# A two-layer graph network on one core: attention in blocks of 512 queries, exponentials over four tiles, and a block's order written as one string

## The chip, the cores and the metric

The kernel runs on one core of a Trainium2 chip. The time is device time in microseconds, from the launch of the program on the core to its end. Every run of the kernel before is given; the median of the three is the number that the change is compared with. The profile is of one more execution of the same program.

The core has five instruction streams that run side by side and wait for one another by semaphores: TensorE (PE, with its weight loads shown apart as PEld), VectorE (DVE), ScalarE (ACT), GpSimd (POOL) and SyncE (SP, which here only issues DMAs). Each stream does its instructions in the order in which the program gives them, so one that waits holds up all that stand behind it on its engine.

## The reference

`x` is 3327 x 128, `adj` is a 3327 x 3327 matrix of zeros and ones. Layer 0 is a graph convolution with a batch norm and layer 1 an attention with `adj` added twice to its scores. Layer 1 takes almost all of the time:

```python
h = max(layernorm(x), 0)
q = (h @ Wq.T).reshape(128, 3327, 8)      # 128 batches d, 3327 nodes n, 8 features h
k = (h @ Wk.T).reshape(128, 3327, 8)
v = (h @ Wv.T).reshape(128, 3327, 8)
a = einsum('dnh,dmh->dnm', q, k) * 128 ** -0.5
a = softmax(a + adj + adj, axis=2)
out = einsum('dnm,dmh->dnh', a, v).reshape(3327, 1024)
x = x + out @ Wo.T
```

So there are 128 independent attentions over 3327 nodes, each with only 8 features, and 128 x 3327 x 3327 exponentials (1.4 thousand million).

## The kernel before

Layer 0 and the first projections fill about the first 260 us of the profile. Everything after is `attention()`.

**Tiles.** The nodes are padded to NP = 3328 = 26 key chunks of 128. Four batches (G = 4) are worked at a time, which makes 32 groups `i`. Inside a group the queries are cut into blocks `y` of QB = 480: six of 480 and a last one of 448. For one key chunk `c` and one half of the four batches (`half`, two batches) there is one *pair*: two score matmuls (`product`, L804), one for each batch, into a PSUM tile `s` of two banks (bank x takes batch x of the half). The contraction has 32 rows (8 features, each as two parts of query and key), so batch b sits on rows 32b to 32b+31 of the array. A block has 26 x 2 = 52 pairs, a group 7 x 52 = 364, each of 960 (or 896) columns on 128 partitions.

**Two ways through a pair.** Chunks 0 to 17 (`WC = 18`) are *plain*: DVE adds the adjacency tile `at` to the scores and writes a slice of a tile `d` (`add`, L939), and ACT later takes exp(2x) over the whole `d` in place (`late`, L984). Chunks 18 to 25 are *weighted*: ACT takes exp(2x) straight from PSUM into a tile `f` (`weighted`, L948), and POOL multiplies `f` by a tile `wt` of exp(2 adj) that was stored in DRAM (`wd`) beforehand (L951). Either way the pair ends in SBUF, and four matmuls in four column groups (`weigh`, L686) multiply two pairs by the values and a column of ones into the accumulator bank `av`.

**Steps.** A block is 13 steps (`SU = NC // 2`) of four pairs. Ten steps have three plain pairs and one weighted, and the three steps in `DOUBLE = (3, 7, 11)` have two of each. The text of a step fixes the order on every engine:

```python
weighted(rest[0][0], coming)          # score product, exp (ACT), multiply (POOL)
late()                                # ACT: exp over the d of the step before, 2 or 3 pairs
add(0, product(...)); second(0)       # DVE add; PE: four weigh matmuls, three steps behind
add(1, product(...))
add(2, product(...))                  # or a second weighted()
second(1)
```

**Buffers.** PSUM is full: `psc` has three `s` tiles of two banks, used in turn by every `product` whichever kind it is, and two banks hold `av`, one for each of two blocks in turn. In SBUF there are four `d` (three pairs each), six `f`, four `at` (two chunks each) and three `wt` (one chunk each). A product therefore waits until the pair three places before it has been read, by DVE if that was plain and by ACT if it was weighted.

**Beside it.** `fetch(x + PRE)` issues the `at` and `wt` DMAs from SP two steps ahead. `finish` (L696 to L720) turns a finished block's `av` on DVE, divides it and stores it; its parts are placed at the steps in `PARTS`. `loads` brings the next group's q, k and v, with POOL sorting k (`sort`, L193), spread over the group. `begin` and `go_on` place ten small pieces in a group (six projections of a later part of layer 1 and four of the output product; L209 to L295): a matmul into the idle `av` bank, a copy on DVE, and for q and k two more instructions on POOL and DMAs from SP. `more_weights` does exp on chunks 24 and 25 of the next block's `wd`, in the first group only.

Of the kernel before, what the change touches and what calls it, by code (L numbers as in the profile page):

```python
# [9 lines left out]
F32 = mybir.dt.float32  # L10
# [11 lines left out]
P = 128  # L22
NC = 26
# [3 lines left out]
QB = 480  # L27
# [4 lines left out]
SU = NC // 2  # L32
# [4 lines left out]
DOUBLE = (3, 7, 11)  # L37
PARTS = (3, 7, 8)
# [9 lines left out]
def tile_two_layer_gnn(  # L48
# [73 lines left out]
    PRE = 2  # L122

    FROM = [3 * SU] + [LAG + 1] * (NG - 1)

# [565 lines left out]
    def finish(rp, av, d0, n0, w):  # L691
# [10 lines left out]
        ri = av[:, QB : QB + J]  # L702
# [22 lines left out]
    def attention():  # L725
# [3 lines left out]
        with tc.tile_pool(name="exd", bufs=4) as ep, tc.tile_pool(  # L729
            name="adj", bufs=4  # L730
        ) as ap, tc.tile_pool(name="adw", bufs=3) as wp, tc.tile_pool(
            name="exf", bufs=6
# [7 lines left out]


# [4 lines left out]
            if True:  # L746
                steps = [
                    (i, y, s)
                    for i in range(NG) for y in range(len(qblocks)) for s in range(SU)
                ]  # L750

                def at(i):
                    return i * G

                def pairs(s):


                    return kinds[s]

                kinds = []  # L760
                for s in range(SU):
                    j, k = (sum(len(x[i]) for x in kinds) for i in range(2))
                    n = 2 if s in DOUBLE else 1
                    kinds.append((
                        [(x // 2, x % 2) for x in range(j, j + 4 - n)],
                        [(WC + x // 2, 1 - x % 2) for x in range(k, k + n)],
                    ))


                wanted, have = [], {}  # L770
                for x, (i, y, s) in enumerate(steps):
                    n0, w = qblocks[y]
                    for c, _ in pairs(s)[0]:
                        if (0, i, y, c // 2) not in have:
                            have[0, i, y, c // 2] = None
                            wanted.append((x, 0, i, y, c // 2))
                    for c, _ in pairs(s)[1]:
                        if (1, i, y, c) not in have:
                            have[1, i, y, c] = None
                            wanted.append((x, 1, i, y, c))  # L780

                def fetch(x):
                    while wanted and wanted[0][0] <= x:
                        _, kind, i, y, c = wanted.pop(0)
                        n0, w = qblocks[y]
                        if kind:
                            a = wp.tile([P, QB], F32, name="wt")
                            nc.sync.dma_start(a[:, :w], wd[c - WC, :, n0 : n0 + w])
                        else:
                            a = ap.tile([P, 2, QB], F32, name="at")  # L790
                            n = min(2, WC - 2 * c)
                            nc.sync.dma_start(
                                a[:, :n, :w], adjr[:, 2 * c : 2 * c + n, n0 : n0 + w]
                            )
                        have[kind, i, y, c] = a

                def product(i, y, c, half):
                    q, k, _ = sets[i % 2]
                    n0, w = qblocks[y]
                    we = w + w % 2  # L800
                    p = psc.tile([P, 2, NB], F32, name="s")
                    for x in range(2):
                        rs = slice(64 * half + 32 * x, 64 * half + 32 * x + 32)
                        nc.tensor.matmul(  # L804
                            p[:, x, :we], k[rs, c, :], q[rs, n0 : n0 + we],
                            start=True, stop=True,
                        )
                    return p

                waiting, ending, pending = [], [], []  # L810
                others = [
                    args for b in range(G)
                    for args in q_loads(sets[0][0], 32 * b, b, NB, NP - NB)
                ]
                late = None

                def more_weights(i, y, s):

                    if i or y + 1 >= len(qblocks) or s not in (1, 8, 12):
                        return  # L820
                    n0, w = qblocks[y + 1]
                    if s == 1:
                        have["w"] = wk.tile([P, 2, QB], F32, name="t4")
                        nc.sync.dma_start(
                            have["w"][:, :, :w], adjr[:, WC + NW :, n0 : n0 + w]
                        )
                    a = have["w"][:, :, :w]
                    if s == 8:
                        nc.scalar.activation(a, a, AF.Exp, bias=low, scale=2.0)
                    if s == 12:  # L830
                        nc.sync.dma_start(
                            wd[NW:, :, n0 : n0 + w].rearrange("c p n -> p c n"), a
                        )

                extra, begun = [], []

                def begin(i, y, s):
                    if extra and s in DOUBLE[1:]:  # L840
                        begun.append(extra.pop(0))
                        drive(begun[0], avs2[(i * len(qblocks) + y + 1) % 2])

                def go_on(i, y, s):
                    if begun and s in DOUBLE:
                        drive(begun[0])
                    elif begun:
                        drive(begun.pop(0))
                    for j in [1, 2] if i == 0 else [i + 2] if i + 2 < NG else []:
                        if (y, s) != (2 * (j - 1) if i == 0 else 0, 3):  # L850
                            continue
                        hj = wk.tile([P, CH], F32, name="hj")
                        nc.sync.dma_start(hj, hd[:, j * CH : (j + 1) * CH])
                        extra.extend(projections(wk, hj, j, False, ov, low_half[:CH, 1:2]))
                    if (y, s) == (2, 12) and i:
                        extra.extend(outputs(wk, i - 1))

                def second(part):

                    if not due:  # L860
                        return
                    (i, y, s), es = waiting[0]
                    n0, w = qblocks[y]
                    av = avs2[(i * len(qblocks) + y) % 2]
                    ps = sum(pairs(s), [])
                    for j in (0, 1) if part == 0 else (2, 3):
                        c, half = ps[j]
                        for x in range(2):
                            weigh(
                                sets[i % 2], av, w, es[j][:, x, :w], 2 * half + x, c,  # L870
                                s == 0 and part == 0, s == SU - 1 and part == 1,
                            )
                    if part:
                        waiting.pop(0)
                        if s == SU - 1:
                            ending.append(finish(rp, av, at(i), qblocks[y][0], w))

                def step():
                    for g in ending[:1]:
                        if next(g, g) is g:  # L880
                            ending.pop(0)

                def first(x):
                    i, y, s = steps[x]
                    return product(i, y, *pairs(s)[1][0])

                def first_loads():

                    q, k, v = sets[0]
                    ks = sets[1][1].rearrange("p c n -> p (c n)")  # L890
                    for b in range(G):
                        for args in k_loads(ks, 32 * b, b, 0, NP):
                            nc.sync.dma_start(*args)

                    for b in range(G):
                        for args in q_loads(q, 32 * b, b, 0, NB):
                            nc.sync.dma_start(*args)
                    for args in v_loads(v, 0):
                        nc.sync.dma_start(*args)

                    for c, copy in (
                        (16, nc.scalar.copy), (0, nc.vector.tensor_copy),
                        (4, nc.gpsimd.tensor_copy), (8, nc.scalar.copy),
                        (20, nc.vector.tensor_copy), (12, nc.gpsimd.tensor_copy),
                        (24, nc.vector.tensor_copy),
                    ):
                        n = min(4, NC - c)
                        copy(
                            k[:, c : c + n, :],
# [286 lines left out]
```

## Time and profile before

| | |
|---|---|
| runs | 10039.32, 10042.86, 10046.28 us; median 10042.86 |
| profiled execution | span 10038.4 us from its first to its last instruction; no other time is recorded for it, and the three runs lie 0.9 to 7.9 us above this span |
| busy: ACT, PE, DVE, POOL | 9869.9 (98%), 9683.1 (96%), 9306.6 (93%), 8455.3 us (84%) |
| TensorE clock granted | 0.995 of full speed as a mean |
| attention: first and last DVE add | 268.8 and 10010.9 us |
| instructions of the four main lines | L939 DVE 8064, L951 POOL 3584, L984 ACT 2912, L948 ACT 3584 |

A row of the groups reads: line, engine, operation, output tile <- input tiles, partitions x elements of output and input, count, then busy time in all and the mean of one, then the time the engine sat idle just before such an instruction and what ended most of that. The record of one instruction can overlap that of the next on its engine; busy time counts such a stretch once, the mean counts it in both. Matmuls are pipelined, so PE's busy share is not its share of peak.

### The profile page before, as it was taken

How to read it: one execution, taken by the hardware profiler on the slowest of the kernel's cores; microseconds unless marked ns; L12 is line 12 of the kernel's file. 1: busy time of each engine (PE TensorE's matmuls, PEld its weight loads, DVE VectorE, ACT ScalarE, POOL GpSimd, SP SyncE). 2: the span in 40 equal slices, each digit the busy share in tenths (PEclk: the TensorE clock that was granted, in tenths of full speed). 3: DMA queues.
4: the chain of work that ended last, by engine and by line, in shares of the span. 5: the costliest groups of instructions: out<-in, count | busy, mean ns of one | idle time of the engine just before them, and what ended most of it. 6: DMA issues, size and time to landing. Idle time of an engine off the chain costs nothing. (4 is left out here: it accounts for less than half of the span.)

```text
span 10038.4 us, 187289 instructions
## 1 busy us (share of the span) xinstructions
PE 9683.1 (96%) x71535; PEld 2727.4 (27%) x71535; DVE 9306.6 (93%) x9527; ACT 9869.9 (98%) x6649; POOL 8455.3 (84%) x4331
## 2 busy tenths in 40 slices
PE   8899999999999999999999999999999999999998
PEld 3222222222222222222222222222222222222222
DVE  5899999999999999999999999999999999999998
ACT  5999999999999999999999999999999999999999
POOL 1788888888888888888888888888888888888887
PEclk9999999999999999999999999999999999999999
DMA  7766666666666666666666666666666666666654
GB/s 296 197 181 170 168 168 174 173 172 167 165 173 174 172 169 167 166 175 174 171 167 170 167 171 176 169 169 167 169 175 172 172 166 167 171 175 172 161 156 131
DMA packets 1035388, 1735.65 MB, mean 173 GB/s; under 512 B 126926, under 2 KB 1009356, under 8 KB 1025132
## 3 DMA queue, kind: packets, MB, share of 16 engines
q1 hardware_dynamic: 1031975, 1718.70, 62.4%
q8 instruction: 562, 9.21, 0.4%
q0 software_dynamic: 784, 4.03, 0.1%
q14 instruction: 351, 2.87, 0.1%
q10 hardware_dynamic: 1716, 0.85, 0.0%
HBM read 1620.93 MB, written 102.27 MB: 172 GB/s over the span
## 5 line engine op out<-in xcount | busy, mean ns | idle before, releaser
L939 DVE SCALAR_TENSOR_TENSOR d<-at,s 128x960 f32<-128x960 f32 x8064 | 8730.2, 1138 | 430.2 <-PE s L804 291.0
L951 POOL TENSOR_TENSOR f<-f,wt 128x960 f32<-128x960 f32 (+1 forms) x3584 | 7936.6, 2233 | 1339.1 <-ACT f L948 1305.4
L984 ACT ACTIVATE d<-d 128x2880 f32<-128x2880 f32 (+1 forms) x2912 | 7071.9, 2429 | 6.9 <-DVE d L939 4.8
L686 PE MATMUL av<-d,v 128*9 128x480 f32 x32256 | 5050.8, 565 | 0.6 <-ACT d L984 0.6
L804 PE MATMUL s<-q,k 32*128 32x480 f32 x23296 | 4236.3, 475 | 288.5 <-ACT f L948 210.9
L948 ACT ACTIVATE f<-s 128x960 f32<-128x960 f32 (+1 forms) x3584 | 3445.0, 988 | 18.4 <-issue 8.7
L804 PEld LDWEIGHTS s<-q,k 32*128 32x128 f32 x23296 | 1806.3, 182 | 5528.9 <-DVE d L939 3409.2
L686 PE MATMUL av<-f,v 128*9 128x480 f32 x14336 | 2842.4, 565 | 0.0
L686 PEld LDWEIGHTS av<-d,v 128*9 128x9 f32 x32256 | 584.2, 88 | 1204.8 <-issue 1203.1
L686 PEld LDWEIGHTS av<-f,v 128*9 128x9 f32 x14336 | 317.4, 88 | 153.6 <-issue 140.0
L193 POOL CAST k<-ks 128x256 fp32r<-128x256 f32 x434 | 284.0, 654 | 0.0
L517 PE MATMUL acc<-a,A 128*128 128x512 f32 (+1 forms) x364 | 159.1, 591 | 22.7 <-DMA a<-in_adj 22.7
L240 POOL TENSOR_TENSOR o<-pf,o 104x512 fp32r<-104x512 f32 x124 | 159.8, 1289 | 9.9
L696 DVE STREAM_TRANSPOSE avs<-av 128x480 f32<-128x480 f32 (+1 forms) x224 | 149.3, 667 | 4.4 <-PE av L686 4.4
L527 DVE TENSOR_REDUCE amax<-a 128x1 f32<-128x3327 f32 x26 | 93.7, 3605 | 53.9 <-DMA a<-in_adj 53.9
L495 POOL TENSOR_SCALAR heavy<-heavy 128x3328 f32<-128x3328 f32 x6 | 17.8, 2960 | 128.5 <-DMA heavy<-in_adjT 80.3
L517 PEld LDWEIGHTS acc<-a,A 128*128 128x128 f32 x364 | 71.5, 200 | 113.7 <-issue 97.9
L524 ACT ACTIVATE junk<-a 128x3327 bf16<-128x3327 f32 x26 | 77.3, 2972 | 19.9 <-DMA a<-in_adj 19.9
L238 DVE TENSOR_SCALAR pf<-av,low_half 104x512 f32<-104x512 f32 x62 | 46.5, 751 | 37.4 <-PE av L209 36.3
L236 DVE COPY pf<-av 104x512 f32<-104x512 f32 x62 | 42.9, 691 | 39.5 <-PE av L209 38.8
L239 POOL CAST o<-pf 104x512 fp32r<-104x512 f32 x124 | 76.0, 613 | 0.0
L215 DVE COPY ov<-av 104x512 f32<-104x512 f32 x62 | 42.9, 691 | 33.4 <-PE av L209 33.3
(133 smaller groups left out, 913.7 us busy)
## 6 DMA issues: line engine op xcount, KB each, us to landing
at<-in_adjT SPq DMA_DIRECT2D x1728, 480.0 KB
wt<-wd SPq DMA_DIRECT2D x1536, 240.0 KB
at<-in_adjT SPq DMA_DIRECT2D x288, 448.0 KB
wt<-wd SPq DMA_DIRECT2D x256, 224.0 KB
ks<-kT SPq DMA_DIRECT2D x496, 104.0 KB
q<-qT SPq DMA_DIRECT2D x496, 104.0 KB
a<-in_adj SPq DMA_DIRECT2D x26, 1663.5 KB
kT<-o SPq DMA_DIRECT2D x128, 208.0 KB
```

Of the source, the lines that this page charges most:

```text
L193: nc.gpsimd.tensor_copy(k[:, c : c + n, half * 64 : half * 64 + 64], ks.bitcast(F32).rearrange("g (p c) -> g c p", c=NC)[:, c : c + n, :],)
L240: nc.gpsimd.tensor_tensor(o[:CH, 1], f[:CH], of[:CH, 0], ALU.subtract)
L517: nc.tensor.matmul(acc[i][:, :w], A[:, c, :], a[:, n0 : n0 + w], start=(c == 0), stop=(c == NC - 1),)
L524: nc.scalar.activation(junk, a[:, :N], AF.Copy, accum_out=deg[:, c : c + 1])
L527: nc.vector.tensor_reduce(amax[:, c : c + 1], a[:, :N], AX.X, ALU.max, apply_absolute_value=True)
L686: nc.tensor.matmul(av[32 * b : 32 * b + H + 1, :w], tiles[2][:, b, c, :], e, start=first, stop=last,)
L696: nc.vector.transpose(avs[:, :J, :].rearrange("p j h -> p (j h)"), av[:, : 32 * J].rearrange("p (q j) -> p j q", j=J),)
L804: nc.tensor.matmul(p[:, x, :we], k[rs, c, :], q[rs, n0 : n0 + we], start=True, stop=True,)
L939: nc.vector.scalar_tensor_tensor(d[:, j, :, :w], have[0, i, y, c // 2][:, c % 2, :w] .unsqueeze(1).to_broadcast([P, 2, w]), SAFE / 2, p[:, ...
L948: nc.scalar.activation(f[:, :, :w], p[:, :, :w], AF.Exp, scale=2.0)
L951: nc.gpsimd.tensor_tensor(f[:, :, :w], f[:, :, :w], have[1, i, y, c][:, :w].unsqueeze(1).to_broadcast([P, 2, w]), ALU.mult,)
L984: nc.scalar.activation(flat, flat, AF.Exp, scale=2.0)
```

## The change

The block is now 512 queries: six blocks of 512 and a last one of 256. In the last one two key chunks lie side by side in a tile, so that every tile of scores, and every instruction on one, has 2 x 512 columns. A block of 512 has 52 such tiles and the block of 256 has 26. `RUN = 4` plain tiles share a `d`, so the exponential over `d` has 4096 columns. There are three `d` instead of four (each larger by a third and by 512/480), and five `f` instead of six.

The steps are gone. A string names what comes next, one for the blocks of 512 (`WIDE`) and one for the last (`NARROW`): `A` a plain tile, `B` a weighted tile, `L` the exponential over the oldest full `d`, `v` the value matmuls of the oldest couple of tiles of one kind, `F` and `G` parts of `finish`, `P` the matmul of one of the small pieces and `E` the rest of it (its DMAs come at the next `L`). A `v` lies six couples behind (`BEHIND`). `at` and `wt` tiles are fetched by how many tiles of their kind have gone by (`AHEAD`); a `wt` tile of the last block holds two chunks. In `finish` the reciprocal is written over the first columns of `av`, since the bank is now full. The diff, cut to its core (what the removed steps did is described above):

```diff
-QB = 480
+QB = 512
-SU = NC // 2
-DOUBLE = (3, 7, 11)
-PARTS = (3, 7, 8)
+RUN = 4
+BEHIND = 6
+AHEAD = ((8, 3), (4, 2))
+WIDE = (
+    "LAAvABvvABvAAvALAvFBBvABAvAALAvB"
+    "AvALAvGBvBAAvLAAvvBAvALAvPABAvAA"
+    "LvvABBvBEALAvAAPvBLAAvAAvBvBE"
+)
+NARROW = "ABvAAAvLvBAvAAAvLvBBFvABAvAALvABALvAAvvBGABALv"
...
-        ri = av[:, QB : QB + J]
+        ri = av[:, :J]
...
-        with tc.tile_pool(name="exd", bufs=4) as ep, tc.tile_pool(
+        with tc.tile_pool(name="exd", bufs=3) as ep, tc.tile_pool(
...
-            name="exf", bufs=6
+            name="exf", bufs=5
...
+NY = len(qblocks)
+many = [QB // w for _, w in qblocks]
+orders = [WIDE if m == 1 else NARROW for m in many]
+def items(kind, y):
+    first, units = ((0, WC), (WC, NC - WC))[kind]
+    m = many[y]
+    return [
+        (first + u * m, half ^ kind) for u in range(units // m) for half in (0, 1)
+    ]
...
+def fetch(kind, ahead):
+    queue = wanted[kind]
+    while (
+        issued[kind] < len(queue)
+        and queue[issued[kind]][0] <= number[kind] + ahead
+        and issued[kind] <= max(current[kind], 0) + AHEAD[kind][1]
+    ):
...
+def product(i, y, c, half):
+    q, k, _ = sets[i % 2]
+    n0, w = qblocks[y]
+    p = psc.tile([P, 2, NB], F32, name="s")
+    for e in range(many[y]):
+        for x in range(2):
+            rs = slice(64 * half + 32 * x, 64 * half + 32 * x + 32)
+            nc.tensor.matmul(
+                p[:, x, e * w : (e + 1) * w],
+                k[rs, c + e, :], q[rs, n0 : n0 + w],
+                start=True, stop=True,
+            )
+    return p
...
+def put(kind, i, y, item):
+    couple[kind].append(item)
+    if len(couple[kind]) == 2:
+        quads.append((i, y, list(couple[kind])))
+        couple[kind].clear()
+def exponentials():
+    d, n = full.pop(0)
+    flat = d[:, :n].rearrange("p j x n -> p (j x n)")
+    nc.scalar.activation(flat, flat, AF.Exp, scale=2.0)
+def second():
+    i, y, two = quads.pop(0)
+    n0, w = qblocks[y]
+    m = many[y]
+    av = avs2[(i * NY + y) % 2]
+    z = done[i, y] = done.get((i, y), -1) + 1
+    end = orders[y].count("v") - 1
+    for e in range(m):
+        for c, half, t in two:
+            for x in range(2):
+                weigh(
+                    sets[i % 2], av, w, t[:, x, e * w : (e + 1) * w],
+                    2 * half + x, c + e, z == 0 and e == 0,
+                    z == end and e == m - 1,
+                )
+    if z == end:
+        ending.append(finish(rp, av, at(i), n0, w))
...
+def plain(i, y, j):
+    c, half = items(0, y)[j]
+    fetch(0, AHEAD[0][0])
+    number[0] += 1
+    current[0] += j % 4 == 0
+    p = product(i, y, c, half)
+    if not open_:
+        open_.append(ep.tile([P, RUN, 2, QB], F32, name="d"))
+    d, z = open_[0], len(open_) - 1
+    open_.append(j)
+    nc.vector.scalar_tensor_tensor(
+        d[:, z],
+        have[0, i, y, j // 4][:, j // 2 % 2]
+        .unsqueeze(1).to_broadcast([P, 2, QB]),
+        SAFE / 2, p, ALU.min, ALU.add,
+    )
+    if z + 1 == RUN or j + 1 == len(items(0, y)):
+        full.append((d, z + 1))
+        open_.clear()
+    put(0, i, y, (c, half, d[:, z]))
+def weighted(i, y, j):
+    c, half = items(1, y)[j]
+    fetch(1, AHEAD[1][0])
+    number[1] += 1
+    current[1] += j % 2 == 0
+    p = product(i, y, c, half)
+    f = fp.tile([P, 2, QB], F32, name="f")
+    nc.scalar.activation(f, p, AF.Exp, scale=2.0)
+    nc.gpsimd.tensor_tensor(
+        f, f,
+        have[1, i, y, j // 2].unsqueeze(1).to_broadcast([P, 2, QB]),
+        ALU.mult,
+    )
+    put(1, i, y, (c, half, f))
...
+        for token in orders[y]:
+            if token == "A":
+                plain(i, y, z[0])
+                z[0] += 1
+            elif token == "B":
+                weighted(i, y, z[1])
+                z[1] += 1
+            elif token == "L":
+                if full:
+                    exponentials()
+                for part in then:
+                    part()
+                then.clear()
+            elif token == "F":
+                step()
+            elif token == "G":
+                step()
+                then.append(step)
+            elif token == "P":
+                if extra:
+                    begun.append(extra.pop(0))
+                    drive(begun[0], avs2[(i * NY + y + 1) % 2])
+            elif token == "E":
+                if begun:
+                    drive(begun[0])
+                    then.append(lambda part=begun.pop(0): drive(part))
+            else:
+                if i * total_v + v >= BEHIND:
+                    second()
+                if v == start and i + 1 < NG:
+                    pending = loads(sets[(i + 1) % 2], at(i + 1), ksp)
+                    total = len(pending)
+                while pending and (total - len(pending)) * (
+                    total_v - start - 10
+                ) <= (v - start) * total:
+                    pending.pop(0)()
...
```

## The prediction

> **What bounds the kernel now.** First the page's busy shares, then busy time by stretch, to see whether ACT's 98% is 98% everywhere.
>
> ```profile
> PE 9683.1 (96%) x71535; PEld 2727.4 (27%) x71535; DVE 9306.6 (93%) x9527; ACT 9869.9 (98%) x6649; POOL 8455.3 (84%) x4331
> ```
> ```profile
> 0.00:250.00 250.00, 201.22 (x506) 94.38 (x507) 146.06 (x246) 137.95 (x144) 47.39 (x61) 0.91 0.79 297
> ...
> 1000.00:5000.00 4000.00, 3896.18 (x29220) 1080.55 (x29212) 3767.04 (x3818) 3998.59 (x2672) 3463.45 (x1765) 1.00 0.63 170
> 5000.00:9000.00 4000.00, 3895.80 (x29230) 1082.16 (x29226) 3766.74 (x3821) 3998.78 (x2673) 3460.47 (x1762) 1.00 0.63 170
> ```
>
> Columns: stretch, length, busy us (count) of PE, PEld, DVE, ACT, POOL, then clock, DMA share, GB/s. ACT idles 2.6 us in 8000, so the attention lasts as long as ACT's instructions do. PE's 97% is not such a bound: the timeline has eight value matmuls in 0.99 us and four score matmuls in 0.49 to 0.89, about 2.5 of the 3.34 us of a step; the rest is waiting.
>
> ACT's price per instruction comes from starts in its timeline (start, record length, what):
>
> ```profile
> 5013.71 2.61 ACT L984 ACTIVATE d<-d 128x2880 f32<-128x2880 f32 x1
> 5016.21 1.83 ACT L948 ACTIVATE f<-s 128x960 f32<-128x960 f32 x2
> 5017.91 1.83 ACT L984 ACTIVATE d<-d 128x1920 f32<-128x1920 f32 x1
> 5019.60 0.99 ACT L948 ACTIVATE f<-s 128x960 f32<-128x960 f32 x1
> 5020.45 2.64 ACT L984 ACTIVATE d<-d 128x2880 f32<-128x2880 f32 x1
> ```
>
> From start to next start: 2.50 us for 2880 columns, 0.85 for an `f` of 960, 1.69 for 1920. Records are longer than this because they overlap. Means over 1500 to 3500 us: 2.502 (2880), 2.339 (2688), 1.695 (1920), 1.590 (1792), `f` 0.850 (960) and 0.796 (896). The slope over the `d` rows is 0.838 ns a column (it is 0.82 to 0.85 between neighbours), which leaves 0.085 us fixed in each `d`.
>
> Next to ACT stands DVE; its rows and what it and PE wait for:
>
> ```profile
> L939 DVE SCALAR_TENSOR_TENSOR d<-at,s 128x960 f32<-128x960 f32 x6912 | 7546.5, 1148 | 330.9 <-PE s L804 206.3 <-issue 21.0 <-ACT d L984 0.8
> L951 POOL TENSOR_TENSOR f<-f,wt 128x960 f32<-128x960 f32 x3072 | 6864.9, 2253 | 1161.6 <-ACT f L948 1128.3 <-DMA wt<-wd 7.4
> ```
> ```profile
> PEld s L804 <- DVE d L939: 3409.2, 5381, 1.6
> PEld s L804 <- ACT f L948: 1302.6, 1792, 2.0
> DVE d L939 <- PE s L804: 291.0, 604, 2.6
> ACT f L948 <- PE s L804: 6.6, 7, 1.5
> ```
>
> Score matmuls wait for DVE or ACT to free a PSUM tile, DVE waits now and then for scores, ACT almost never.
>
> **The change part by part.** *ACT.* Counts in a group: before, 91 `d` (60 of 2880, 18 of 1920, 10 of 2688, 3 of 1792) and 112 `f` (96 of 960, 16 of 896); after, from the strings, 58 `d` of 4096, one of 2048, and 104 `f` of 1024. The columns are the same, 346,112. Before: 60x2.502 + 18x1.695 + 10x2.339 + 3x1.590 + 96x0.850 + 16x0.796 = 303.2 us (5345 ACT instructions in 8000 us are 26.33 groups of 203, so 303.8 was seen). After, a `d` of 4096 is 2.502 + 1216 x 0.000838 = 3.52, of 2048 1.80, an `f` 0.904: 204.2 + 1.8 + 94.0 = 300.0. Saved: 3.1 a group, 98 us in 32. The Trainium skill (ScalarE: Activation LUTs, What ACT_TABLE_LOAD costs) has 0.833 ns a column and 186 ns fixed less 93 of overlap: 93 x 1280 instructions fewer (40 a group) = 119 us. With its column price the trace leaves (303.8 - 288.4)/203 = 76 ns fixed as a mean, not 93: 97 us. I take the trace. Bounds: 73 us if the 1216 columns past 2880 cost 0.849 each, 122 if all that the trace has above 0.833 is per instruction (50 ns an `f`, 108 a `d`).
>
> *DVE.* Back-to-back adds of 960 start 1.065 us apart (timeline: 5009.11, 5010.17, 5011.24), 1.00 of it columns; at 1024, 1.133. A group has 234 instead of 252: 265 us against 268, still under ACT.
>
> *Order.* What must hold is that ACT is never kept waiting, so I walk `WIDE` with ACT back to back: L 3.52, B 0.904, 46.2 us a block. A product n waits until tile n-3 has been read. From the end of an add to the start of an add on the freed tile takes 0.68 us (DVE record 0.08 beyond the spacing; 0.06 to the matmul, 12.38 to 12.44 in the timeline; matmul 0.51 at 512; 0.03). From a B it is 0.78. Zero is the block's first L. B1 ends at 4.43, B2 5.33, L2 8.86, B3-5 11.57, L3 15.1, B6 16.0, L4 19.5, B8 21.3, L5 24.9, B9 25.8, L6 29.3, B10 30.2, L7 33.7, B11-13 36.4, L8 40.0, B14 40.9, L9 44.4, B16 46.2. On DVE: A5 cannot start before 5.21 (B1's tile); A8 ends 9.75, `F` (0.71) 10.46, A12 15.0, A16 19.5, `G` (0.6) 20.2, A20 24.8, A24 29.3, A28 33.8, then A29 waits for B11's tile until 35.41 (an `E` copy of 0.7 fits here), A32 39.95, A36 44.5, next A4 3.7. Each L needs its fourth add: A12 15.0 for L4 at 16.0, A16 19.5 for 21.3, A20 24.8 for 25.8, A24 29.3 for 30.2, A28 33.8 for 36.4, A32 39.95 for 40.9. Margins are 0.9 us or more, and DVE has two pauses of 1.5 us to recover in. The tight spot is B5: its product needs B3's tile, ready 10.55 for 10.67. I put 5 us in all on such places.
>
> *PE.* Matmul and column counts are the same (728 + 728 a group). A `v` waits for its L: v4 for L1 (3.5; the next product is free only at 5.2), v7 for L2 (8.9; next at 9.8), v16 for L5 (24.9). None holds a product that ACT needs. In `NARROW` a product is four matmuls of 256, the two chunks on the same 32 rows. The Trainium skill (TensorE: Matmul & The Clock Gate, Part 3, The mechanism) lets a weight load overlap running matmuls only in another row group, which speaks against this: each of the 26 products would lay bare one load more. The load's row is 182 ns: 4.7 us a group if bare. The walk of `NARROW` has A12 at 14.8 to 15.2 for an L at 16.0 and PE idle a quarter of the time, so 0 by trace; by the rule, if nothing covered it, up to 150 us in 32 groups. No row of before shows it; I take 0 and keep a part in the range.
>
> *POOL.* 104 x 2.39 (2.253 at 960, 2.116 at 896, so 137 ns per 64 columns) = 249 us a group, as now; sorts and projections add 17. After B11-13 POOL runs behind until 2.8 us into the next block, f16's `v` comes at 7.4. With an `E` of q or k (0.61 + 1.29) f16 ends at 4.7. Five `f`: B6 at 15.1 needs f1, freed by v9 at 13.9. Three `d`: A21 at 25.1 needs v14 at 23. Cost 0; cover gone, each late `v` is ACT's wait one to one.
>
> *SP.* It waits in order: `wt` of couple t+2 for POOL on couple t-1, then 7 to 12 us before need; `at` two tiles ahead (8 adds, about 10 us). The DMAs of an `E` at the next L1 hold SP until about 6.6, so the `at` of A9 (10.4) has 4 us for 512 KB: at worst late by 1 us, twice a group, inside A12's margin. Today SP waits 4429 us for POOL and `wt` is late by 7.4 us in all. Small pieces, `finish` (one column block larger), start and end: 0 to 5 us either way.
>
> Sum: on the profiled execution's span 10038.4 - 98 + 5 = 9945; the median lies 4.5 us above the span, so **9950**.
>
> **Rivals.** *(1) Waits eat half.* Every block idles ACT 0.2 us (B5, the first `v` behind an L, `NARROW`): 224 x 0.2 = 45 more, 9995. For: three PSUM tiles in strict turn under a 3.5 us L. Against: ACT waited 6.6 us in the whole trace with the same three.
>
> *(2) DVE becomes the bound, slower than before.* The 1.133 holds where the next add stands ready and records overlap by 0.08; if each product comes just in time, an add costs its whole record, 1.146 + 0.067 = 1.213. Then A5 to A24 take 20 x 1.213 + 0.71 + 0.6: A24 ends 30.8 for L7 at 30.2, and A20 25.9 for 25.8, so ACT waits 0.57 us in each `WIDE` block: 192 x 0.57 = 109, against 98 saved: 10042.9 + 11 = 10054. It decides at 98/192 = 0.51 us a block, an add of about 1.21. Against it: eleven adds in 12.32 us (1.117 each, small waits included).
>
> *(3) No gain.* An L of 4096 costs more than the rows give: 0.053 us more each (3.57; 0.88 ns for each column past 2880) is 98 us over 1856 of them, so 10043, and the case is within 20 us of today. For: the slope creeps up, 0.82 then 0.849. Against: 0.849 reaches only a quarter of that.
>
> **How the numbers follow.** A difference under 0.2% (20 us) is about what a measurement of this kernel cannot tell from none. ACT-bound as worked out, 9925 to 9965: 0.69. Rival 1, 9965 to 10022: 0.15. Rival 3, within 0.2%: 0.05. Rival 2, slower: 0.11. So faster 0.84, same 0.05, slower 0.11. The range takes the 122 us bound at the low end (9921, less 3 for the ends) and rival 1 at the high end up to 10005.
>
> **What would show it.** Right: ACT busy 99.9% in mid-span with 5216 attention instructions, `d` of 4096 starting 3.52 us before its follower, a group of 300 us, DVE adds 1.13 apart with two pauses a block. Wrong: ACT idle before L (released by DVE: rival 2), before `f` (released by PE: rival 1), a `d` of over 3.55 us (rival 3), or ACT idle in `NARROW` blocks alone (the weight loads).

## The result, and the profile after

The changed kernel takes 10263.19 us (median of four runs, 10259.38 to 10273.62) against 10042.19 for the kernel before (four runs): a ratio of 1.0222, with an interval of 1.0207 to 1.0236. It is 2.2% slower. The forecast was 9950, with a range that ended at 10005. The profiled execution took 10259.38 us with a span of 10257.6.

The busy shares of the page, and busy time by stretch (columns as before: stretch, length, busy us and count of PE, PEld, DVE, ACT, POOL, then clock, DMA share, GB/s):

```profile
PE 9354.4 (91%) x71535; PEld 2593.0 (25%) x71535; DVE 9213.6 (90%) x8951; ACT 9830.7 (96%) x5369; POOL 8402.1 (82%) x4075
```
```profile
1000.00:5000.00 4000.00, 3675.18 (x28588) 1001.47 (x28580) 3645.43 (x3500) 3892.76 (x2099) 3362.85 (x1623) 0.98 0.57 166
5000.00:9000.00 4000.00, 3674.33 (x28552) 1001.50 (x28544) 3642.05 (x3497) 3892.07 (x2096) 3363.29 (x1622) 0.98 0.57 167
```

ACT idled 2.6 us of these 8000 before; now it idles 215. ACT is still the engine with the most work, but it is kept waiting. The groups with their shapes kept apart, and then the waits, say for what:

```profile
L874 ACT ACTIVATE d<-d 128x4096 f32<-128x4096 f32 x1856 | 6737.5, 3630 | 7.1 <-DVE d L937 5.8 <-ACT f L956 0.8
L956 ACT ACTIVATE f<-s 128x1024 f32<-128x1024 f32 x3328 | 3287.7, 1034 | 260.3 <-PE s L814 212.9 <-POOL f L957 25.2 <-POOL k L195 1.6
```
```profile
ACT f L956 <- PE s L814: 212.9, 191, 5.2
DVE d L937 <- DMA at<-in_adjT: 149.5, 81, 3.9
```

The exponential over `d` never waits (7.1 us in all). The one from PSUM waits 212.9 us for scores, in long pieces: 191 times, up to 5.2 us. The last row is new. `at` held DVE for 0.8 us in the whole profile of before, and for 149.5 us here.

The waits are not spread evenly. Lined up by the order string over 26 groups, ACT idles 8.4 us a group, and about 6 of that stand in front of one token: `B6`, in block 1 (2.2 us) and block 2 (3.9 us) of every group. In these two blocks the `E` of the block before has left its DMAs to the first `L`: they are the second halves of the `k` and `q` pieces. Here is one of them in the timeline, a block 1 whose first `L` starts at 4999.76. SP first, then POOL, DVE, ACT and PE (start, length, engine, line, what; in brackets idle time and what ended it; on PE, `x4` of L814 is two products and `x8` of L688 one `v`):

```profile
5000.45 0.37 SPq L789 DMA_DIRECT2D wt<-wd  x1
5004.81 1.71 SPq L248 DMA_DIRECT2D kT<-o  x2
5006.61 0.40 SPq L799 DMA_DIRECT2D at<-in_adjT  x1
```
```profile
5004.17 0.61 POOL L241 CAST o<-pf 104x512 fp32r<-104x512 f32 x1
5004.86 1.28 POOL L242 TENSOR_TENSOR o<-pf,o 104x512 fp32r<-104x512 f32 x1
```
```profile
5009.56 0.71 DVE L698 STREAM_TRANSPOSE avs<-av 128x512 f32<-128x512 f32 x1
5012.21 6.87 DVE L937 SCALAR_TENSOR_TENSOR d<-at,s 128x1024 f32<-128x1024 f32 x6 [1.94 <-DMA at<-in_adjT]
```
```profile
4999.76 3.64 ACT L874 ACTIVATE d<-d 128x4096 f32<-128x4096 f32 x1
...
5011.54 3.61 ACT L874 ACTIVATE d<-d 128x4096 f32<-128x4096 f32 x1
5017.66 1.02 ACT L956 ACTIVATE f<-s 128x1024 f32<-128x1024 f32 x1 [2.51 <-PE s L814]
```
```profile
5011.04 1.04 PE L688 MATMUL av<-d,v 128*9 128x512 f32 x8
5013.48 0.51 PE L814 MATMUL s<-q,k 32*128 32x512 f32 x4 [1.40 <-DVE d L937]
5014.61 0.50 PE L814 MATMUL s<-q,k 32*128 32x512 f32 x2 [0.62 <-DVE d L937]
5015.04 1.79 PE L688 MATMUL av<-f,v 128*9 128x512 f32 x8
5016.76 0.91 PE L814 MATMUL s<-q,k 32*128 32x512 f32 x4
```

Read from the top: SP issues a `wt` at 5000.45 and then stands still for four microseconds, because its next instruction, a store of `kT`, needs what POOL copies at 5004.17. Two more instructions of the store go out at 5004.81, and only then, at 5006.61, does SP ask for the `at` of `A9` to `A12`. DVE starts `A9` at 5012.21, 5.6 us after the request and after 1.94 us of idle time. The products of `A11` and of `A13` need the tiles that `A9` and `A10` free, so PE has two pauses, of 1.40 and 0.62 us. Then comes a `v`, which takes 1.79 us where the others take 1.04, and only behind it the scores of `B6`, for which `A11` had to free the tile. ACT idles 2.51 us before `B6`. In block 2 it is worse: DVE idles 1.9 us before `A9` of block 1 and 3.0 before that of block 2, as means over the 26 groups.

Two things lengthen this. The transfer itself shares the DMA engines with all that SP had held back; and the clock that PE is granted falls after its pauses, to half for some three microseconds:

```profile
5000.00:5004.00 4.00, 3.76 (x40) 0.84 (x32) 3.26 (x4) 4.00 (x2) 4.00 (x2) 1.00 0.97 261
...
5008.00:5012.00 4.00, 3.50 (x26) 0.80 (x24) 2.27 (x3) 3.94 (x5) 4.00 (x3) 1.00 0.99 278
5012.00:5018.00 6.00, 3.98 (x26) 1.02 (x26) 5.79 (x6) 3.49 (x2) 5.82 (x3) 0.77 1.07 290
5015.30:5018.50 3.20, 3.20 (x20) 0.53 (x12) 3.20 (x4) 0.84 (x1) 2.52 (x2) 0.50 1.09 282
```

The last three columns of these stretches are clock, DMA share and GB/s: the DMA engines are full from 5008 to 5018, and the clock is 0.77 in the six microseconds of the wait, 0.50 in the stretch that holds the slow `v`. Over the whole kernel it is 0.977, before it was 0.995.

### The profile page after: what moved, and what is told of

Read it like the earlier page. It is cut to its first block, busy times and chain, and to the rows that moved or that the text cites. A ratio compares the mean times of both kernels' runs of the same rounds, so it can differ in the third digit from the quotient of the medians.

```text
span 10257.6 us, 180643 instructions
## 1 busy us (share of the span) xinstructions
PE 9354.4 (91%) x71535; PEld 2593.0 (25%) x71535; DVE 9213.6 (90%) x8951; ACT 9830.7 (96%) x5369; POOL 8402.1 (82%) x4075
## 4 chain that ended last, share of the span: by engine, by line
ACT 27%; PE 14%; issue 9%; DVE 7%; POOL 5%; DMA 3%; SPq 0%; DVEq 0%; ACTq 0%; POOLq 0%
ACT d L874 20%; PE av L688 8%; ACT f L956 7%; DVE d L937 7%; PE s L814 5%; POOL f L957 4%; DMA at<-in_adjT 3%; POOL o L242 1%; PE av L211 0%; PE av L288 0%; POOL o L241 0%; DMA att<-oq 0%; SPq L248 0%; DVE av L707 0%; POOL k L195 0%
## 5 line engine op out<-in xcount | busy, mean ns | idle before, releaser
L937 DVE SCALAR_TENSOR_TENSOR d<-at,s 128x1024 f32<-128x1024 f32 x7488 | 8637.7, 1215 | 876.6 <-PE s L814 375.3
L957 POOL TENSOR_TENSOR f<-f,wt 128x1024 f32<-128x1024 f32 x3328 | 7878.6, 2393 | 1594.7 <-ACT f L956 1594.3
L874 ACT ACTIVATE d<-d 128x4096 f32<-128x4096 f32 (+1 forms) x1888 | 6795.0, 3601 | 7.1 <-DVE d L937 5.8
L814 PE MATMUL s<-q,k 32*128 32x512 f32 x23296 | 3845.1, 474 | 743.3 <-DVE d L937 506.7
L688 PE MATMUL av<-d,v 128*9 128x512 f32 x32256 | 3947.4, 573 | 95.6 <-ACT d L874 94.8
L956 ACT ACTIVATE f<-s 128x1024 f32<-128x1024 f32 x3328 | 3287.7, 1034 | 260.3 <-PE s L814 212.9
L814 PEld LDWEIGHTS s<-q,k 32*128 32x128 f32 x23296 | 1559.4, 184 | 5515.6 <-DVE d L937 3254.4
L688 PE MATMUL av<-f,v 128*9 128x512 f32 x14336 | 1779.4, 575 | 0.0
L688 PEld LDWEIGHTS av<-d,v 128*9 128x9 f32 x32256 | 532.9, 89 | 1163.6 <-issue 771.0
L688 PEld LDWEIGHTS av<-f,v 128*9 128x9 f32 x14336 | 273.5, 89 | 642.4 <-issue 536.3
L698 DVE STREAM_TRANSPOSE avs<-av 128x512 f32<-128x512 f32 (+1 forms) x224 | 150.0, 670 | 6.1 <-PE av L688 6.1
L288 PE MATMUL av<-wo,t 128*104 128x128 f32 x512 | 73.2, 288 | 0.0
```

What stands on the lines that cost most here:

```text
L288: nc.tensor.matmul(bank[:CH, :D], tT[:, e, :CH], wo[:, e, :], start=(e == 4 * i), stop=(e == 4 * i + 3),)
L688: nc.tensor.matmul(av[32 * b : 32 * b + H + 1, :w], tiles[2][:, b, c, :], e, start=first, stop=last,)
L698: nc.vector.transpose(avs[:, :J, :].rearrange("p j h -> p (j h)"), av[:, : 32 * J].rearrange("p (q j) -> p j q", j=J),)
L814: nc.tensor.matmul(p[:, x, e * w : (e + 1) * w], k[rs, c + e, :], q[rs, n0 : n0 + w], start=True, stop=True,)
L874: nc.scalar.activation(flat, flat, AF.Exp, scale=2.0)
L937: nc.vector.scalar_tensor_tensor(d[:, z], have[0, i, y, j // 4][:, j // 2 % 2] .unsqueeze(1).to_broadcast([P, 2, QB]), SAFE / 2, p, ALU.mi ...
```

## The experiments

Each kernel was compared with the kernel before, which ran on the same chip at 10041 to 10044 us. A "loss" is how much longer ACT takes from the start of one instruction to the start of the next than it does when nothing is late (3.508 us after a `d` of 4096, 0.9025 after an `f`), added up per block and averaged over the groups. Losses are read from the one profiled execution of each kernel; that of e1_ahead12 took 10035.50 us and that of e5_v7 10084.12, which lie 8 below and 17 above their medians.

**1. Is it SP? Two independent edits: ask for `at` earlier, or store later.**

```diff
-AHEAD = ((8, 3), (4, 2))
+AHEAD = ((12, 3), (4, 2))
```

> Only the reach of the at fetch changes, from 8 to 12 adds ahead, so the at of the third d tile of a block is asked for in the block before, ahead of the stores of the small piece. Theory S (those stores hold SP behind POOL, and the at asked for behind them lands 2 to 4 us late): ACT's idle time at B6 of blocks 1 and 2 (6.0 us a group) is gone, a group falls from 311 to about 305 us, time about 10263 - 190 = 10070; granted clock back above 0.99. Theory B (three PSUM tiles in strict turn under an exponential of 3.5 us): B6 still waits, time within 20 us of 10263. Theory D (DMA as a whole is too slow for the pattern): the wait for at moves to another tile, time over 10200.

And, with `AHEAD` as it was, the DMAs of an `E` moved from the next `L` to the one behind it:

```diff
 for part in then: part()
 then.clear()
+then.extend(later)
+later.clear()
...
-then.append(lambda part=begun.pop(0): drive(part))
+later.append(lambda part=begun.pop(0): drive(part))
```

> Only the place of a small piece's last part (its DMAs) changes, from the next L to the L after it; the reach of the fetch is as in the changed kernel. Theory S: SP reaches the store after it has asked for the at of A9 and A13, so B6's wait in blocks 1 and 2 goes as in the run with the longer reach: about 10070. Theory B: no change, 10263 within 20. Theory D: as for the longer reach, over 10200.

e1_ahead12 took 10043.59 us (ratio 1.0002, 0.9994 to 1.0011) and e2_store_l2 10045.65 (1.0007, 0.9998 to 1.0016). Either edit alone takes back 218 to 220 us, where 190 were expected, and the losses in front of `B6` are gone in both; the theory that SP is the cause holds and its rivals fall. The clock is back at 0.995 in both profiled executions. Windows and waits of e1_ahead12:

```profile
1000.00:5000.00 4000.00, 3710.91 (x29202) 1021.07 (x29202) 3724.57 (x3583) 3979.32 (x2147) 3444.73 (x1662) 1.00 0.59 171
5000.00:9000.00 4000.00, 3711.01 (x29202) 1021.46 (x29202) 3722.54 (x3581) 3978.66 (x2145) 3438.81 (x1657) 1.00 0.59 170
```
```profile
ACT f L956 <- PE s L814: 33.3, 105, 3.3
DVE d L937 <- DMA at<-in_adjT: 0.6, 1, 0.6
```
```profile
SPq L248 <- POOL o L241: 864.2, 124, 9.6
SPq L799 <- DVE d L937: 1295.0, 983, 4.2
```

The pair of SP's own waits is the instructive one. SP still stands 864.2 us in front of the stores (853.7 in the changed kernel), but nobody behind it is in need: the `at` request has gone out before, and now it waits for a free `at` tile (1295.0 us, against 189.2), which is as early as four tiles allow. That the same bytes cost nothing when asked for four adds earlier also says that the DMA engines have room enough.

**2. Is it the turn of the PSUM tiles at the two `B` in front of `A9`?** In `WIDE` and in `NARROW` one `A` and one `B` change places; once with `AHEAD` as changed, once with that of e1_ahead12.

```diff
-"...ALAvFBBvABAvAALAvB"
+"...ALAvFBBvBAAvAALAvB"
```

> Only the strings change: the first three B of a block stand together, BBvBA instead of BBvABv, so the third B takes the tile of an add (A8) and not that of the first B. Theory T (B5's product comes 0.1 to 0.2 us late in every block because it takes B3's tile in turn): the 0.23 us after B3 in each block goes, 1.5 us a group, 50 us in all: about 10215. Theory S alone: no change at this place, 10263 within 20, and B6's waits of blocks 1 and 2 stay at 6 us a group.

> Both the longer reach and the new place of the third B. Theory S with T: the two add up, 10263 - 190 - 50 = about 10025, a group of 303.5 us, at the time of the kernel before. Theory S alone: 10070. Theory B: over 10200.

e3_bbb took 10289.89 us (1.0249, 1.0231 to 1.0266), e4_ahead_bbb 10048.68 (1.0008, 0.9999 to 1.0017). The waits in front of `B6` stay (2.3 and 3.7 us), and the small loss at the `B`s themselves only falls from 0.23 to 0.18. This theory falls. That e3_bbb is 27 us slower than the changed kernel, and e4_ahead_bbb 5 slower than e1_ahead12, fits neither theory and was not followed up.

**3. What is left: 94 us between e1_ahead12 and the forecast.** With SP out of the way a group takes 303.8 us, as long as before, although ACT's own instructions add up to 58 x 3.508 + 1.80 + 104 x 0.9025 = 299.1. The 4.7 us of loss stand in every block: 1.57, 0.68, 0.68, 0.32, 0.94, 0.35 and 0.19. The windows above show only 42 us of idle time in 8000, 1.6 a group. The rest hides inside busy time, as these four rows of e1_ahead12 show:

```profile
5054.60 1.02 ACT L956 ACTIVATE f<-s 128x1024 f32<-128x1024 f32 x1
5055.52 3.62 ACT L874 ACTIVATE d<-d 128x4096 f32<-128x4096 f32 x1
5059.03 1.01 ACT L956 ACTIVATE f<-s 128x1024 f32<-128x1024 f32 x1
5060.04 3.62 ACT L874 ACTIVATE d<-d 128x4096 f32<-128x4096 f32 x1
```

From the first `f` to the `d` behind it it is 0.92 us, from the second 1.01, its whole record. An instruction that is not ready in time loses the overlap first, up to 0.11 us, and no view counts that as idle.

What makes them late is PE. Here are `B3`, `B4` and `B5` of a block 3 of e1_ahead12, ACT and then PE:

```profile
5599.20 3.06 ACT L956 ACTIVATE f<-s 128x1024 f32<-128x1024 f32 x3
```
```profile
5599.60 1.05 PE L688 MATMUL av<-d,v 128*9 128x512 f32 x8
5600.58 1.13 PE L814 MATMUL s<-q,k 32*128 32x512 f32 x6
```

Back to back the three would take 2 x 0.9025 + 1.02 = 2.83 us; they take 3.06. The product of `B5` needs the tile of `B3`, whose record ends about 5600.25. But PE is at a `v` that began at 5599.60, and the next products, `B5`'s among them, start at 5600.58. It is so nearly everywhere. Of the 4.7 us a group, 4.1 lie in single losses of 0.03 us and more (groups 3 to 28, each laid beside PE's records; for an `L`, the product of its fourth add). For 3.6 us of these PE came to the product straight from a `v`, for 0.4 from a matmul of a small piece, and for 0.02 it had been idle; and the freed tile had by then lain waiting long enough to account for 3.7 of the 4.1.

These are e1_ahead12's groups on PE:

```profile
L688 PE MATMUL av<-d,v 128*9 128x512 f32 x32256 | 3884.2, 564 | 92.7 <-ACT d L874 91.8
L814 PE MATMUL s<-q,k 32*128 32x512 f32 x23296 | 3826.2, 467 | 650.2 <-DVE d L937 404.7 <-ACT f L956 173.6 <-DMA q<-qT 26.9
L688 PE MATMUL av<-f,v 128*9 128x512 f32 x14336 | 1739.4, 563 | 0.0
```

A block of 512 has 26 `v` of four value matmuls and the last block 13 of eight half as wide: 728 a group, 23296 in all; the rows of L688 count 46592. So a value matmul (`v` is a tile of F32) leaves two records and a score matmul (q and k are F32R) one, the "x8" of the timeline is one `v`, and four value matmuls cost 4 x (3884.2 + 1739.4)/23296 = 0.97 us as a mean over both widths (1.04 at 512 in the timeline), not half of that. All three rows together are 9450 us (some of it counted twice, since records overlap: the page has PE busy for 9226.6): PE has little room. The next kernels test what that means. The first moves one `v` of a block from in front of `A9` and `B5` to behind them, the second halves the columns of every value matmul (`w // 2`, half of the value product is left out).

```diff
-"...ALAvFBBvABAvAALAvB"
+"...ALAvFBBABvAvAALAvB"
```

> The kernel with the longer reach, and in the string of the blocks of 512 one v moved back by two tokens, from before A9 and B5 to behind them. Theory V: the 0.23 us that a block loses at the first three B gets less, but the v of 0.9 us now stands ahead of A10 and of later products, so most comes back at B6 or B9: 10044 within 30, with less lost at B3 to B5 and more behind. Theory T2 (only this one v is badly placed): 0.23 x 6 x 32 = 44 us faster, 10000.

> The kernel with the longer reach of the fetch, and every value matmul over half of its columns (256 instead of 512, 128 in the last block); the other half of the queries gets no sum, and the denominators are held at 1 or more. It leaves half of the value product out. Theory V (what is left of the missing gain, 4.7 us a group over ACT's own 299, is PE: a v takes 0.9 us of PE and not the 0.4 of the forecast, so products of B stand behind a v and come late): with v at about 0.45 the products come in time, a group falls to 299 to 300.5 us, time about 10044 - 32 x 4 = 9915. Theory B (the three PSUM tiles in turn, or the coupling of ACT and DVE, which half a value matmul leaves as they are): a group stays within 1 us of 303.8 and the time within 30 of 10044.

e5_v7: 10067.41 us (1.0026, 1.0015 to 1.0038). The loss at the `B`s falls from 0.24 to 0.05 and comes back as 0.5 to 0.8 in front of `B6` in four of the blocks: where a `v` stands decides which product is late, and moving it only moves the loss.

e6_half_v: 10722.84 us (1.0692, 1.0656 to 1.0728), which neither theory had foreseen. This run doesn't measure what it was made for. The page's row of granted clock, the clock of two neighbouring stretches (the number before the last two), waits, and PE's timeline:

```profile
PEclk8677677767677766666766766666767666677665
```
```profile
5003.00:5009.80 6.80, 5.28 (x52) 1.87 (x44) 6.32 (x7) 6.80 (x6) 6.13 (x3) 1.00 0.43 132
5009.80:5020.00 10.20, 10.15 (x68) 3.07 (x68) 7.74 (x9) 9.94 (x7) 8.09 (x5) 0.50 0.52 171
```
```profile
ACT f L956 <- PE s L814: 548.1, 1038, 3.0
```
```profile
5004.99 0.62 PE L688 MATMUL av<-d,v 128*9 128x256 f32 x8
...
5010.81 1.04 PE L688 MATMUL av<-d,v 128*9 128x256 f32 x8
5011.78 0.79 PE L814 MATMUL s<-q,k 32*128 32x512 f32 x2
```

The same eight records take 0.62 us at one place and 1.04 six microseconds later. With less to do PE was granted a lower clock (0.692 as a mean), and then scores came late 1038 times. The Trainium skill (TensorE: Matmul & The Clock Gate, Part 1) knows two clocks, full and half, with half after an idle window of about 3.4 us. The two clocks are in this trace, but no such window: between 1000 and 9000 us PE waits 688.5 us for tiles, in 1350 pauses of half a microsecond as a mean, and none is over 1.6. Of many short pauses between groups of matmuls that were enough for the clock to swing, the skill tells in the same part (A second HAM failure mode: psum-queue depth-cycling), and that is what this trace looks like. How much pause it takes, no run here shows.

**4. New orders, and the places of two buffers in SBUF.** e7_strings has three new strings on top of `AHEAD` (12, 3): `FIRST` for a group's block 0, `WIDE` for blocks 1 to 5, `NARROW` for the last. e8_layout also exchanges the places of the pool of `f` and of `qk1`.

```diff
+FIRST = (
+    "AvLAvABvABAvAALvABvFBABvAAvAAvLB"
+    "AvLAAvBGvBLAAvAvABAvALvAABvAPAAv"
+    "LvBABvAEBBvAAvAPAALvvALAvBBEv"
+)
 WIDE = (
-    "LAAvABvvABvAAvALAvFBBvABAvAALAvB"
-    "AvALAvGBvBAAvLAAvvBAvALAvPABAvAA"
-    "LvvABBvBEALAvAAPvBLAAvAAvBvBE"
+    "LAAvvABAvBALAvABvAvBBFAvAAALvvBA"
+    "AvAAvGLBvBAAvAAvvLBAvLAAvBAPAvAL"
+    "AvvBABvBEALAvAvABPAvLAAAEvBvB"
 )
-NARROW = "ABvAAAvLvBAvAAAvLvBBFvABAvAALvABALvAAvvBGABALv"
+NARROW = "ABvAAvALBvAvLAAvBAvBABvAAvALBLvAAvAAvBAFvLGABv"
```

> The kernel with the longer reach and three new strings, the first block of a group with its own, in which a v (0.9 us of PE) or a P (1.05 us) stands ahead of a B's product only where that product has over 1 us to spare, and three B no longer follow each other. Theory V: half or more of the 4.7 us a group comes back, a group of 301 to 302 us, 9955 to 9990. Theory B: strings that keep three PSUM tiles and the long exponential gain nothing, within 30 us of 10044.

> As the new strings, and the pool of f opened after that of the second q and k, so that the first load of k no longer lies over a tile that layer 0's last DMAs still read. Theory M (place in SBUF delays the start: the first add comes at 277 us where it came at 269): first add at 269 to 271, the time 7 to 9 us below that of the new strings. If the start hangs on something else: within 3 us of it.

e7_strings took 10272.42 us (1.0230, 1.0213 to 1.0247), e8_layout 10259.09 (1.0217, 1.0200 to 1.0234). Blocks 1 to 5 do lose less (0.28 to 0.47 us) and the last 0.04, but block 0 loses 9.6. The waits of e8_layout name it:

```profile
ACT f L961 <- PE av L693: 200.4, 32, 7.3
ACT f L961 <- PE s L819: 104.2, 116, 9.2
```

Once a group an `f` waits about 6 us for a `v` (`av`, L693) to give back one of the five `f` tiles: `FIRST` keeps a `v` of weighted tiles too far behind. Is it `FIRST` alone? e9_nofirst uses the new `WIDE` in block 0 as well, e10_oldfirst the changed kernel's `WIDE` there; e11_layout is e1_ahead12 with the exchange of the two pools only:

```diff
-        ) as ep, ... name="exf", bufs=5) as fp, tc.tile_pool(name="qk1", bufs=1) as qkp1, ...
+        ) as ep, ... name="qk1", bufs=1) as qkp1, tc.tile_pool(name="exf", bufs=5) as fp, ...
```

> The string FIRST of block 0 is gone: blocks 0 to 5 all follow the new WIDE, the last block the new NARROW, with AHEAD 12 and the pool of f opened after qk1. Theory F (the whole loss of e8_layout lies in FIRST, and the new WIDE and NARROW are good): blocks 1 to 5 keep their 0.28 to 0.47 us of loss and the last 0.04, block 0 goes from 9.6 us to at most 1.6 as in e1_ahead12: 10259 - 32 x 8.0 = about 10003 if the rest of the group is as in e8_layout, and down to 9965 if block 0 is no worse than the other blocks. Rival (block 0 has a cause of its own, whatever its string: the first v of a group come behind NARROW's last tiles and run out of f): block 0 still loses 5 us or more, 10110 and over.

> As e8_layout, but block 0 follows the string WIDE of the changed kernel, in place of FIRST; blocks 1 to 5 and the last keep the new strings. Theory F: block 0 loses 1.6 us as in e1_ahead12, and the blocks behind it 0.28 to 0.47: about 10003 or a little less, and less than e11_layout by 32 x 1.2 = 40. Rival (a loss that is taken out of one block comes back in the next): the group stays at 303.8 as in e1_ahead12, and the time is that of e11_layout.

> As e1_ahead12 with one edit alone: the pool of f is opened after qk1, so that the places of the two in SBUF are exchanged. Theory M (the first load of k waits for what still uses its place): the first add moves from 277 to about 263 us and the time from 10044 to about 10030, the group staying at 303.8. Rival (the start is set by something else, and the 13 us of e8_layout came from its strings): 10044.

e9_nofirst took 10124.61 us (1.0082, 1.0069 to 1.0096). e10_oldfirst 10142.38 (1.0098, 1.0083 to 1.0114). Block 0 still loses 5.6 and 6.1 us, so the theory that all of the loss lay in `FIRST` was wrong; but 4 us did. The same old string loses 1.67 in e11_layout, and 6.1 in e10_oldfirst, where it follows the new `NARROW`. The losses are waits for scores at `B1`, `B2` or `B4`, at the start of the block. So the suspicion falls on this `NARROW`: it loses almost nothing itself, but would hand its `v`s to block 0. Section 5 tests it.

e11_layout: 10034.82 us (0.9990, 0.9981 to 0.9999), 8.8 less than e1_ahead12, with the group unchanged at about 304. The start tells why. SP's timeline of the changed kernel, and then that of e11_layout:

```profile
232.77 0.87 SPq L789 DMA_DIRECT2D wt<-wd  x1
258.77 3.58 SPq L906 DMA_DIRECT2D k<-kT  x8
```
```profile
233.85 0.78 SPq L789 DMA_DIRECT2D wt<-wd  x1
243.08 3.58 SPq L906 DMA_DIRECT2D k<-kT  x8
```

In front of the first load of `k` the changed kernel's SP waits for a DMA of layer 0 that stores `xs` (to `xd`):

```profile
SPq L906 <- DMA xd<-xs: 24.8, 1, 24.8
```

The load waits for what last used its place in SBUF, and the new sizes of `d` and `f` had moved that place onto memory that layer 0 still needed. This wait is gone in e11_layout, which asks for the load 15.7 us earlier than the changed kernel; the steady run of adds starts 9.1 us earlier (269.49 against 278.60 in e1_ahead12). 3.87 us of the rest go into a wait for scores behind the first add.

**5. What works, put together.** e12_wide_only is e11_layout with the new `WIDE` in blocks 1 to 5, the changed kernel's `WIDE` in block 0 and its `NARROW` in the last.

> As e11_layout, but blocks 1 to 5 of a group follow the new WIDE of e7_strings; block 0 keeps the changed kernel's WIDE and the last block its NARROW. Theory N (the 5 us that block 0 lost in e9_nofirst and e10_oldfirst come from the new NARROW in front of it, which passes value matmuls on): block 0 is back at 1.6 us, blocks 1 to 5 fall from 0.67, 0.67, 0.35, 0.97, 0.35 to 0.42, 0.44, 0.28, 0.47, 0.31, so the group falls by 1.1 us to 302.8 and the time by 35 us to about 10000, under both kernels. Rival (the new WIDE in block 5 passes the work on through the last block all the same): block 0 loses 3 us or more and the time is 10060 or over.

10011.89 us (8 runs, 10007.23 to 10017.38), a ratio of 0.9972, 0.9961 to 0.9982: faster than both kernels. Block 0 is back at 1.8 us and blocks 1 to 5 lose 0.27 to 0.48, so the losses are 3.9 us a group. As this kernel differs from e10_oldfirst in `NARROW` alone, that string did hand the loss on. The gain over e11_layout is 23 us where 35 were expected: a group is 0.99 us shorter (303.0 for 304.0), but the very first group is 4.2 longer.

```profile
1000.00:5000.00 4000.00, 3731.22 (x29290) 1037.84 (x29288) 3752.36 (x3595) 3985.33 (x2153) 3450.35 (x1665) 1.00 0.60 171
5000.00:9000.00 4000.00, 3728.28 (x29282) 1038.64 (x29282) 3749.49 (x3591) 3984.32 (x2152) 3448.77 (x1662) 1.00 0.60 171
```

ACT's idle time is 30 us in 8000 here. Most of what remains above the 299.1 us of a group is lost overlap.

## Why the prediction was wrong

The time missed is 10263.2 - 9950 = 313 us. The runs split it in two: 219.6 from the changed kernel to e1_ahead12, and 93.6 from e1_ahead12 to the forecast. Two steps failed, one for each.

- ***SP*, the first step that failed (219.6 us, forecast 0).** "Hold SP until about 6.6" was nearly right: in the timeline above SP is free at 5006.52, 6.8 us after the block's first `L` (in block 2 it is 7.4, the middle of 26 groups). The rest of the sentence failed twice. "4 us for 512 KB: at worst late by 1 us" took the transfer for 4 to 5 us; it was 5.6 from request to use, with all that had queued behind the store under way too, and `A9` was 1.9 us late. And "inside A12's margin" asked only for `L4`. The next thing that `A9` feeds is not `L4` but the product three tiles later: `A11` frees the tile of `B6`. By the walk's own numbers `A9` starts at 10.46, so `A11` ends at 13.86 and `B6`'s scores are there at 14.5 for a start at 15.1: 0.6 us of margin, not 1.0, and less once the `v` in front of `B6` is counted. The fall of the clock made that `v` 0.75 us longer still.
- ***Order* and *PE*, the second step that failed (forecast 5 us in all, measured 4.7 us a group).** The walk had each product ready in 0.68 us and no engine but DVE and ACT in its way, and of the `v`s it said "None holds a product that ACT needs". The rows in section 3 show that they do, and e5_v7 that the loss goes where the `v` goes. At `B5`, which the walk had named as the tight spot, the scores were to be there 0.12 us early; with a `v` on PE they are 0.22 to 0.42 us late in every block of 512. This makes up the 93.6 us: 4.7 a group, less 0.9 by which ACT's own instructions were cheaper than forecast, less 0.8 that was in the forecast already (its 5 us, and 0.6 by which a group of before is longer than its own sum), is 3.0, and 96 in 32 groups. It is rival 1 in kind (`B3` to `B5`, `NARROW`), at 0.19 to 1.57 us a block where the rival had 0.2; the rival's 9995 was 49 us too low even with SP mended.
- **The price of a `v`, behind that step.** "Eight value matmuls in 0.99 us", taken as a step's eight, were the eight records of four. "The rest is waiting" and "PE idle a quarter of the time" rest on that. The page of before had said it: 46592 records in the two L686 groups for 23296 instructions, and PE 96% busy. The count of a row has to be divided by the count of the program before a price is taken from it.
- ***NARROW*, weight loads (0 taken, up to 150 by the rule).** The block of 256 loses 0.19 us: 0 was right, but not for the reason given, since PE is busy there for 23.7 of 26.75 us and not idle a quarter of the time. The loads did not lie bare: in e1_ahead12 a product of four matmuls of 256 takes 285.6/832 = 0.34 us of PE, one of two of 512 takes 3540.6/9984 = 0.35. The bound came from reading the four as standing on the same 32 rows; in `product` the two batches alternate, so each load goes to other rows than the matmul just before it.
- ***ACT*.** Right, and a little too cautious: 3.508 us for a `d` of 4096 where 3.52 was forecast, 0.9025 for 0.904, so 299.1 for a group instead of 300.0. Rival 3 falls. (The text's sum for a group of before comes to 303.1, not 303.2, and 3.1 a group to 99 us in 32, not 98; neither bears on the result.)
- ***DVE*.** Right: in e1_ahead12 DVE is busy 7447 of 8000 us, and the exponential over `d` waits 5.8 us for it in the whole trace. Rival 2, the only one on the slower side, falls; the slower side came from a queue that the text had priced at nothing.
- ***POOL* (0).** The 25.2 us of waits for `f` are in the changed kernel and are gone in e1_ahead12, so they were a consequence of SP.
- **Start and end (0 to 5 us either way).** 8.8 us, from the places in SBUF, which no step looked at.

e11_layout, with a group no shorter than before, is some 9 us under the kernel before. The traces place this in the first group: from its first weighted exponential to that of the next group it is 321.4 us before and 313.2 in e11_layout. Why that group became shorter stays open.

## What to carry to other kernels

When a step with DMAs is moved on an engine that issues them in order, ask what the first DMA waits for and which request stands behind it; then follow that request to the nearest user, which may be another engine's buffer in turn and not the consumer that the margin was worked out for. Ask for such data one use earlier than the walk needs: here the number 12 in place of 8 was worth 220 us. A new order of a full engine has to be priced with every instruction on that engine, and an order that is good inside a block can hand its arrears to the next.

## What the hardware showed that was not expected

- Less work on TensorE made the kernel slower: with half the value columns the granted clock, 1.00 in one stretch and 0.50 in the next, was 0.692 as a mean in place of 0.995, and the time 10723 in place of 10044 us.
- After PE's pauses of 1.40 and 0.62 us a `v` took 1.79 us instead of 1.04, so that a late transfer costs more than its lateness.
- An ACT instruction that comes just late loses up to 0.11 us of overlap with no idle time shown; 3 of the 4.7 us that e1_ahead12 loses in a group are of this kind.
- A change of tile sizes moved another pool onto memory that was still in use, and so put off the first load of `k` by 15.7 us.
